# Layer 1 feed-forward of a decoder kernel: outer products of routes and ranks made transposed from PSUM

## The chip, the cores and the metric

The kernel runs on one core of a Trainium2 chip. A core has five engines with a queue each, worked off in order: PE multiplies matrices (its weight loads, PEld, are listed apart), DVE works on vectors, ACT applies functions, POOL (GpSimd) does general work, and SP issues transfers. The metric is the device time of one execution in microseconds, as the median over several runs.

## The reference

The program is a decoder with twelve steps: in each of four layers a mixer, a cross-attention or the like, and a feed-forward. `x` has 16 blocks of 128 tokens with 256 features. The change touches the sixth step alone, the feed-forward of Layer 1, which adds this to `x` (with the layer-normalised `x` as input):

```
TOPK = 4                                  # A: (64, 16, 256), B: (64, 256, 16), W: (256, 256)
vecs = jnp.einsum('arh,bsh->bsar', A, x)
arrows = jnp.linalg.norm(vecs, axis=-1)
_, idx = jax.lax.top_k(arrows, TOPK)
routes = jax.nn.one_hot(idx, arrows.shape[-1], dtype=x.dtype).sum(-2) / TOPK
v = jnp.einsum('bsa,bsar->bsr', routes, vecs)
delta = jnp.einsum('bsa,ajr,bsr->bsj', routes, B, v)
base = jnp.einsum('bsh,jh->bsj', x, W) + bias
return base + delta
```

For each token there are 64 routes of 16 ranks. The four routes with the longest vectors are chosen; their vectors are summed to `v`, and each chosen route sends `v` through its own matrix of B. So `delta` is one product of 1024 columns (64 routes by 16 ranks) with B, whose left side is the outer product of `routes` and `v`.

## The kernel before

`x` stays on the core, as 128 partitions (tokens) by 16 blocks by 256 features. A group is four blocks (`GB`), 512 tokens. `norm_T(g)` normalises a group and transposes it to `xT` (features on partitions) with PE's transposes and two copies.

`L1_ffn` (L680 to L743) works block by block, in two parts which `overlap` (L115) puts out one block apart: `route(i)`, then `expand(i-1)`.

- `route(i)` (L695): two products of 128x512 in PSUM, `pv`, from `xT` and A (L704). DVE copies them to `vecs` (L705), and ACT squares them to `sq` (L706). DVE sums the squares of each route to `n2` (L708), finds the eight largest and their places (L710, L712), and makes `rt`, a row of 64 zeros and ones (L716, L718). POOL multiplies `vecs` by `rt` (L720), DVE sums that over the routes to `v` (L722, L723), and writes the outer product of `rt` and `v` over `sq`, 128x1024 (L724).
- `expand(i)` (L727): PE transposes the outer product in eight parts to PSUM (`puT`, L732), ACT copies them to `uT` (L733), and one chain of products in PSUM, `pa`, adds W's part, the bias as a product with a row of ones, and eight products with B (L735). `add_x` (L150) adds `pa` to `x` on DVE.

Products of f32 operands appear in the profile as two records each: L92 is the line of the helper `chain` through which most products go, so they are told apart by their tiles. PSUM tiles come from three pools of banks: `mm` with four (`pv`), `tp` with two (all transposes), `ac` with two (`pa`). `vecs`, `sq` and `uT` have two buffers each.

The order of the instructions in each engine's queue isn't the source's order. A planner puts them out when they are ready by its own costs, with the source's order as priority, and inserts the waits. So instructions of neighbouring blocks, and some of the next step (`bn_stats` of Layer 2's first norm, loads of its weights), stand between those of this stage. The helper `Pipe` (L124), which holds back pieces of work for a number of steps, is there already and is used by Layer 2's mixer.

The next step, Layer 2's mixer (`mamba`, L765), starts with `norm_T(0)`, products `pconv` (L833), and small tables `cw`, `nw`, `vec` loaded at L781 to L787.

Of the kernel before, what the change touches and what calls it, by code (L numbers as in the profile page):

```python
# [11 lines left out]
F32 = mybir.dt.float32  # L12
BF16 = mybir.dt.bfloat16
# [4 lines left out]
ALU = mybir.AluOpType  # L18
# [4 lines left out]
P = 128  # L23
NB = 16
S = 128
D = 256
GB = 4
NG = NB // GB
GT = GB * S
# [12 lines left out]
class Decoder:  # L42
# [637 lines left out]
    def L1_ffn(self):  # L680
        nc = self.nc
        NA, R, TOP = 64, 16, 4
        wa = self.load_w("L1_fA", 2, NA * R)
        wb = self.load_w("L1_fB", 8, D)
        ww = self.load_w("L1_fWT", 2, D)
        with ExitStack() as es:
            pool = lambda n, b: es.enter_context(self.tc.tile_pool(name="l1f_" + n, bufs=b, reuse_waits="tile"))
            one, sm, big = pool("1", 1), pool("sm", 3), pool("big", 2)
            bias = one.tile([1, D], F32, tag="bias", name="bias")
            nc.sync.dma_start(bias, self.I["L1_fbias"])  # L690
            count = one.tile([P, NA], F32, tag="count", name="count")
            nc.gpsimd.iota(count, [[1, NA]], base=0, channel_multiplier=0, allow_small_or_imprecise_dtypes=True)
            of = lambda t: t.rearrange("p (a r) -> p a r", a=NA)

            def route(i):  # L695
                xT = self.norm_T(i // GB) if i % GB == 0 else self.l1_xT
                self.l1_xT = xT
                xj = [xT[:, k, self.cols(i % GB)] for k in range(2)]
                vecs = big.tile([P, NA * R], F32, tag="vecs", name="vecs")
                sq = big.tile([P, NA * R], F32, tag="sq", name="sq")  # L700
                for f in range(2):
                    fs = slice(512 * f, 512 * f + 512)
                    pm = self.psum("pv")
                    self.chain(pm, [(xj[k], wa[:, k, fs]) for k in range(2)])  # L704
                    nc.vector.tensor_copy(vecs[:, fs], pm)  # L705
                    nc.scalar.activation(sq[:, fs], pm, AF.Square)  # L706
                n2 = sm.tile([P, NA], F32, tag="n2", name="n2")
                nc.vector.tensor_reduce(n2, of(sq), AX.X, ALU.add)  # L708
                top = sm.tile([P, 8], F32, tag="top", name="top")
                nc.vector.max(top, n2)  # L710
                ix = sm.tile([P, 8], U32, tag="ix", name="ix")
                nc.vector.max_index(ix, top, n2)  # L712
                ixf = sm.tile([P, 8], F32, tag="ixf", name="ixf")
                nc.vector.tensor_copy(ixf, ix)
                rt = sm.tile([P, NA], F32, tag="rt", name="rt")
                nc.vector.tensor_scalar(rt, count, ixf[:, 0:1], None, ALU.is_equal)  # L716
                for k in range(1, TOP):
                    nc.vector.scalar_tensor_tensor(rt, count, ixf[:, k : k + 1], rt, ALU.is_equal, ALU.add)  # L718
                rb = rt.unsqueeze(2).broadcast_to([P, NA, R])
                nc.gpsimd.tensor_tensor(of(vecs), of(vecs), rb, ALU.mult)  # L720
                v = sm.tile([P, R], F32, tag="v", name="v")
                nc.vector.tensor_reduce(v, vecs.rearrange("p (a r) -> p r a", a=NA), AX.X, ALU.add)  # L722
                nc.vector.tensor_scalar(v, v, 1.0 / TOP**2, None, ALU.mult)  # L723
                nc.vector.tensor_tensor(of(sq), rb, v.unsqueeze(1).broadcast_to([P, NA, R]), ALU.mult)  # L724
                return xj, sq

            def expand(i, xj, u):  # L727
                uT = big.tile([P, 8, P], F32, tag="uT", name="uT")
                for f in range(2):
                    pt = self.psum_t("puT")  # L730
                    for k in range(4):
                        nc.tensor.transpose(pt[:, self.cols(k)], u[:, self.cols(4 * f + k)], self.ident)  # L732
                    nc.scalar.copy(uT[:, 4 * f : 4 * f + 4, :].rearrange("p k s -> p (k s)"), pt)  # L733
                pa = self.psum_a()
                self.chain(  # L735
                    pa[:, :D],
                    [(xj[k], ww[:, k, :]) for k in range(2)]
                    + [(self.ones[0:1, :], bias)]
                    + [(uT[:, k, :], wb[:, k, :]) for k in range(8)],
                )  # L740
                self.add_x(i, pa[:, :D])

            self.overlap(NB, route, expand)  # L743


    def softplus(self, pool, z):
# [957 lines left out]
```

## Time and profile before

| what | value |
|---|---|
| median of 3 runs (lowest, highest) | 2934.99 us (2932.88, 2945.16) |
| the profiled execution, time | 2938.75 us |
| the profiled execution, span | 2937.0 us |
| PE, DVE, ACT, POOL busy, share of the span | 86%, 53%, 30%, 28% |
| granted PE clock, mean over the span | 0.885 |
| first instruction on `vecs`, last on `uT` in this stage | 957.0, 1144.3 us |
| L722, sum over routes on DVE, 16 times | 1875 ns mean |
| L724, outer product on DVE, 16 times | 1293 ns mean |
| L708, sums of squares on DVE, 16 times | 1218 ns mean |
| L720, `vecs` by `rt` on POOL, 16 times | 1932 ns mean |
| L705, copy of `vecs` on DVE, 32 times | 682 ns mean |
| L706, square on ACT, 32 times | 604 ns mean |
| L733, copy of `uT` on ACT, 32 times | 591 ns mean |

A profile is one execution as the hardware recorded it. Busy time is what an engine spent in instructions; since matmuls are pipelined and their ends are modelled, a busy PE isn't a PE at its peak. A row of the timeline gives the start in us, the duration in us, the engine, the line, the operation, the tile written and the tiles read with their sizes, how many instructions were merged, and in brackets the idle time before it and what ended that. A row of the waits gives who waited for whom, the sum in us, how often, and the longest.

### The profile page before, as it was taken

Reading aid. Unit: us, or ns where it says so; the run is one execution under the profiler, and the core shown is the slowest. Engines: PE = TensorE matmul, PEld = TensorE weight load, DVE = VectorE, ACT = ScalarE, POOL = GpSimd, SP = SyncE. Lnnn points to the kernel's source line nnn. Section 1 sums busy time; section 2 is a strip of 40 time slices with the busy share of each in tenths; the row PEclk is TensorE's granted clock in tenths of the full one; section 3 lists DMA queues with packets and bytes.
Section 4 is the critical chain, followed back from the end, with each engine's and each line's share of the span. In section 5 each row is a group of like instructions: output and inputs, shape, how many; then the busy total and the mean of one; then the engine's idle time right before and its main releaser. Section 6 shows DMA issues by size and latency. Waiting matters only on the chain. (4 is left out here: it accounts for less than half of the span.)

```text
span 2937.0 us, 33648 instructions
## 1 busy us (share of the span) xinstructions
PE 2523.7 (86%) x12796; PEld 1617.7 (55%) x12796; DVE 1562.2 (53%) x3276; ACT 876.1 (30%) x1590; POOL 827.0 (28%) x880
## 2 busy tenths in 40 slices
PE   7778989989789888889888899399998885979986
PEld 4554444555444555445555566256755565756665
DVE  4998962477533777767676766712245652111110
ACT  1015551256344213433223333121134520111111
POOL 2630110034410212343356666000123314011111
PEclk9898889989788999889799999699888975989998
DMA  4000010000100001000000000200100022132221
GB/s 127 1 25 18 13 44 1 33 1 19 37 1 1 1 1 41 1 1 1 26 7 1 1 1 1 70 1 0 38 1 14 1 71 77 57 80 55 81 55 13
DMA packets 58143, 74.37 MB, mean 25 GB/s; under 512 B 7620, under 2 KB 49669, under 8 KB 57878
## 3 DMA queue, kind: packets, MB, share of 16 engines
q1 hardware_dynamic: 50678, 63.66, 7.0%
q0 software_dynamic: 7296, 8.48, 1.6%
q8 instruction: 103, 1.69, 0.3%
q14 instruction: 66, 0.54, 0.1%
HBM read 55.12 MB, written 18.04 MB: 25 GB/s over the span
## 5 line engine op out<-in xcount | busy, mean ns | idle before, releaser
L1590 POOL DMA_INDIRECT out_dram<-y,xe x40 | 61.9, 1549 | 383.1 <-ACT y L1589 295.9
L1581 DVE TENSOR_TENSOR hT<-sl,pgb 128x320 f32<-128x320 f32 x112 | 54.6, 487 | 194.8 <-PE pgb L92 194.8
L92 PE MATMUL pga<-xeT,e_w1T 128*128 128x320 f32 x448 | 142.4, 441 | 0.0
L92 PE MATMUL pgb<-xeT,e_w3T 128*128 128x320 f32 x448 | 139.8, 435 | 0.0
L92 PE MATMUL pa<-e_w2T,hT 128*128 128x256 f32 x560 | 126.0, 385 | 0.0
L92 PEld LDWEIGHTS pa<-e_w2T,hT 128*128 128x128 f32 x560 | 107.5, 193 | 14.7
L553 DVE TENSOR_TENSOR hT<-sl,pgb 128x512 f32<-128x512 f32 (+1 forms) x56 | 38.4, 686 | 143.0 <-PE pgb L92 137.5
L195 POOL COPY rs<-mv 128x4 f32<-128x4 f32 x48 | 10.8, 227 | 357.7 <-DVE mv L194 357.7
L92 PEld LDWEIGHTS pga<-xeT,e_w1T 128*128 128x128 f32 x448 | 87.0, 196 | 35.0 <-issue 1.4
L92 PEld LDWEIGHTS pgb<-xeT,e_w3T 128*128 128x128 f32 x448 | 86.1, 192 | 36.1 <-issue 1.2
L1580 ACT ACTIVATE sl<-pga 128x320 f32<-128x320 f32 x112 | 48.9, 437 | 190.6 <-PE pga L92 190.6
L1325 POOL TENSOR_TENSOR sc<-sc,mx 128x512 f32<-128x512 f32 x64 | 65.1, 1038 | 132.9 <-DVE mx L1324 81.3
L270 POOL TENSOR_TENSOR prod<-qkv 128x2048 f32<-128x2048 f32 (+7 forms) x24 | 78.0, 3257 | 67.9 <-DVE sc L271 59.8
L198 DVE TENSOR_SCALAR xn<-x,mv,rs 128x256 f32<-128x256 f32 x192 | 80.7, 469 | 28.1 <-POOL rs L102 28.0
L386 PE MATMUL ps<-qb,kT 32*128 32x512 f32 x256 | 80.6, 724 | 13.6 <-ACT pT L391 10.4
L1126 ACT ACTIVATE sc<-sc 128x512 f32<-128x512 f32 x64 | 40.3, 630 | 172.9 <-POOL sc L1125 172.9
L624 PE MATMUL ps<-qb,kn 32*128 32x256 f32 x512 | 87.6, 509 | 4.0 <-DVE kn L610 2.8
L92 PE MATMUL pconv<-xT,w_L_w 128*128 128x512 f32 (+1 forms) x192 | 87.5, 601 | 2.7 <-DVE mt L944 2.2
L1120 PE MATMUL ps<-kk,qq 128*128 128x128 f32 x512 | 73.6, 300 | 17.7 <-POOL qq L1066 17.7
L1120 PEld LDWEIGHTS ps<-kk,qq 128*128 128x128 f32 x512 | 68.1, 210 | 33.8 <-POOL qq L1066 18.7
L630 ACT ACTIVATE pT<-ps 128x512 f32<-128x512 f32 x128 | 67.8, 601 | 62.5 <-PE ps L624 62.4
L193 DVE BATCH_NORM_STATS2 st<-x 128x6 f32<-128x256 f32 x192 | 77.7, 413 | 15.3 <-DMA x<-in_x 6.5
(475 smaller groups left out, 6088.5 us busy)
## 6 DMA issues: line engine op xcount, KB each, us to landing
e_w1T<-in_L_w1T SPq DMA_DIRECT2D x8, 896.0 KB, 6.6
e_w3T<-in_L_w3T SPq DMA_DIRECT2D x8, 896.0 KB, 6.0
e_w2T<-in_L_w2T SPq DMA_DIRECT2D x8, 896.0 KB, 6.3
slots<-blank SPq DMA_DIRECT2D x8, 652.5 KB, 11.3
xe<-slots SPq DMA_DIRECT2D x8, 652.5 KB, 4.1
ct<-in_ctx SPq DMA_DIRECT2D x8, 512.0 KB, 4.6
x<-in_x SPq DMA_DIRECT2D x4, 512.0 KB, 6.6
ctx<-in_ctx SPq DMA_DIRECT2D x16, 128.0 KB, 2.3
```

The lines of the kernel that those rows point to most:

```text
L92: self.nc.tensor.matmul(out, a, b, start=(i == 0), stop=(i == n - 1))
L193: nc.vector.bn_stats(st[:, j, :], self.x[:, g * GB + j, :])
L198: nc.vector.tensor_scalar(xn[:, j, :], self.x[:, g * GB + j, :], mv[:, j, 0:1], rs[:, j : j + 1], ALU.subtract, ALU.mult)
L270: nc.gpsimd.tensor_tensor(prod[:, :k, :], qkv[:, m0 : m0 + k, 256:512], q, ALU.mult)
L386: nc.tensor.matmul(ps[r], kT[rw, j, c, :], qb[rw, j, c].rearrange("p e n -> p (e n)"), start=True, stop=True)
L624: nc.tensor.matmul(ps[r][:, D * c : D * c + D], kn[rw, j, self.cols(c)], qb[rw, j, e], start=True, stop=True)
L630: nc.scalar.activation(pT.rearrange("p c t -> p (c t)"), ps[r], AF.Exp, scale=5.0)
L1120: nc.tensor.matmul(ps[:, self.cols(n)], qq[n][e][:, cs], kk[e][:, cs], start=True, stop=True)
L1325: nc.gpsimd.tensor_tensor(sc, sc, mx.unsqueeze(2).broadcast_to([P, 4, S]), ALU.add)
L1580: nc.scalar.activation(sl, pa[:, :HALF], AF.Silu)
L1581: nc.vector.tensor_tensor(hT[:, f, hs], sl, pb[:, :HALF], ALU.mult)
L1590: nc.gpsimd.indirect_dma_start(out, bass.IndirectOffsetOnAxis(xe[:, t, D + 4 : D + 5].bitcast(I32), 0), y, None, bounds_check=NB * S - 1, ...
```

## The change

The outer product is no longer written with tokens on partitions and then transposed. Per group, `rt` (now bfloat16, kept for four blocks) and `v8` (v divided by 16, repeated eight times to 128 columns) are transposed to `rT` (64 routes by 512 tokens) and `vT` (128 by 512). For each of eight parts of the 1024 columns a product of `member`, a table of zeros and ones in bfloat16, with `rT` spreads eight routes over 128 partitions in PSUM, and DVE multiplies that by `vT` into `uT`. The pieces are held back by `Pipe` and put out over the four blocks after their group. The copies of `vecs` go from DVE to ACT. The bias is loaded to all partitions and added to `x` by POOL, one instruction a group, instead of being a product in each chain. `member` is made once at the stage's start by three POOL instructions.

```diff
-            bias = one.tile([1, D], F32, tag="bias", name="bias")
-            nc.sync.dma_start(bias, self.I["L1_fbias"])
+            bias = one.tile([P, 1, D], F32, tag="bias", name="bias")
+            nc.sync.dma_start(bias[:, 0, :], self.I["L1_fbias"][0].partition_broadcast(P))
+
+            whole = one.tile([NA, 8, 8, R], F32, tag="whole", name="whole")
+            nc.gpsimd.memset(whole, 1.0)
+            nc.gpsimd.affine_select(
+                out=whole, in_=whole, pattern=[[-8, 8], [-1, 8], [0, R]], compare_op=ALU.is_equal, fill=0.0, base=0,
+                channel_multiplier=1,
+            )
+            member = one.tile([NA, 8, P], BF16, tag="member", name="member")
+            nc.gpsimd.tensor_copy(member, whole.rearrange("p f k r -> p f (k r)"))
+            pipe, group = self.Pipe(), {}
...
             def route(i):
-                xT = self.norm_T(i // GB) if i % GB == 0 else self.l1_xT
-                self.l1_xT = xT
-                xj = [xT[:, k, self.cols(i % GB)] for k in range(2)]
+                if i % GB == 0:
+                    group["xT"] = self.norm_T(i // GB)
+                    group["rt"] = sm.tile([P, GB, NA], BF16, tag="rt", name="rt")
+                    group["v"] = sm.tile([P, GB, 8, R], F32, tag="v8", name="v8")
+                    xg = self.x[:, i : i + GB, :]
+                    nc.gpsimd.tensor_tensor(xg, xg, bias.broadcast_to([P, GB, D]), ALU.add)
+                rt, v8 = group["rt"][:, i % GB, :], group["v"][:, i % GB]
+                xj = [group["xT"][:, k, self.cols(i % GB)] for k in range(2)]
...
-                    nc.vector.tensor_copy(vecs[:, fs], pm)
+                    nc.scalar.copy(vecs[:, fs], pm)
                     nc.scalar.activation(sq[:, fs], pm, AF.Square)
...
-                rt = sm.tile([P, NA], F32, tag="rt", name="rt")
...
-                nc.vector.tensor_scalar(v, v, 1.0 / TOP**2, None, ALU.mult)
-                nc.vector.tensor_tensor(of(sq), rb, v.unsqueeze(1).broadcast_to([P, NA, R]), ALU.mult)
-                return xj, sq
-
-            def expand(i, xj, u):
-                uT = big.tile([P, 8, P], F32, tag="uT", name="uT")
-                for f in range(2):
-                    pt = self.psum_t("puT")
-                    for k in range(4):
-                        nc.tensor.transpose(pt[:, self.cols(k)], u[:, self.cols(4 * f + k)], self.ident)
-                    nc.scalar.copy(uT[:, 4 * f : 4 * f + 4, :].rearrange("p k s -> p (k s)"), pt)
...
-                    + [(self.ones[0:1, :], bias)]
...
-            self.overlap(NB, route, expand)
+                nc.vector.tensor_scalar(v8, v.unsqueeze(1).broadcast_to([P, 8, R]), 1.0 / TOP**2, None, ALU.mult)
+
+            def expand(g, xT, rt, v8):
+                rT = big.tile([NA, GT], BF16, tag="rT", name="rT")
+                vT = big.tile([P, GT], F32, tag="vT", name="vT")
+                uT = big.tile([P, 8, GT], F32, tag="uT", name="uT")
+
+                def turn():
+                    pt = self.tp.tile([NA, GT], BF16, tag="tp", name="prT")
+                    for j in range(GB):
+                        nc.tensor.transpose(pt[:, self.cols(j)], rt[:, j, :], self.identb)
+                    nc.scalar.copy(rT, pt)
+                    pv = self.psum_t("pvT")
+                    for j in range(GB):
+                        nc.tensor.transpose(pv[:, self.cols(j)], v8[:, j].rearrange("p k r -> p (k r)"), self.ident)
+                    nc.scalar.copy(vT, pv)
+
+                def outer(fs):
+                    for f in fs:
+                        pu = self.psum_t("pu")
+                        nc.tensor.matmul(pu, member[:, f, :], rT, start=True, stop=True)
+                        nc.vector.tensor_tensor(uT[:, f, :], pu, vT, ALU.mult)
+
+                def sums(js):
+                    for j in js:
+                        pa = self.psum_a()
+                        self.chain(
+                            pa[:, :D],
+                            [(xT[:, k, self.cols(j)], ww[:, k, :]) for k in range(2)]
+                            + [(uT[:, k, self.cols(j)], wb[:, k, :]) for k in range(8)],
+                        )
+                        self.add_x(g * GB + j, pa[:, :D])
+
+                pipe.put(1, turn)
+                pipe.put(2, lambda: outer(range(4)))
+                pipe.put(3, lambda: (outer(range(4, 8)), sums([0])))
+                pipe.put(4, lambda: sums([1, 2, 3]))
+
+            for i in range(NB):
+                route(i)
+                pipe.step()
+                if i % GB == GB - 1:
+                    expand(i // GB, group["xT"], group["rt"], group["v"])
+            pipe.drain()
```

More of the change, by code (lines that the diff above doesn't have):

```diff
@@ L722, in route @@
                 nc.vector.tensor_reduce(v, vecs.rearrange("p (a r) -> p r a", a=NA), AX.X, ALU.add)
-                nc.vector.tensor_scalar(v, v, 1.0 / TOP**2, None, ALU.mult)
-                nc.vector.tensor_tensor(of(sq), rb, v.unsqueeze(1).broadcast_to([P, NA, R]), ALU.mult)
-                return xj, sq
-            def expand(i, xj, u):
-                uT = big.tile([P, 8, P], F32, tag="uT", name="uT")
-                for f in range(2):
-                    pt = self.psum_t("puT")
-                    for k in range(4):
-                        nc.tensor.transpose(pt[:, self.cols(k)], u[:, self.cols(4 * f + k)], self.ident)
-                    nc.scalar.copy(uT[:, 4 * f : 4 * f + 4, :].rearrange("p k s -> p (k s)"), pt)
[L734 to L737, printed above, removed]
-                    + [(self.ones[0:1, :], bias)]
-                    + [(uT[:, k, :], wb[:, k, :]) for k in range(8)],
-                )
-                self.add_x(i, pa[:, :D])
```

## The prediction

> **What bounds the kernel now.** The page's chain of waits is followed back over 2% of the span only, so it doesn't reach the changed stage. I asked for the tiles vecs, uT and rt instead: all lie between 955 and 1145 us. The busy times of that stretch:
>
> ```profile
> core 0: us, PE busy (x) PEld busy (x) DVE busy (x) ACT busy (x) POOL busy (x), PEclk, DMA share, GB/s
> 955.00:1145.00 190.00, 162.50 (x638) 106.64 (x638) 139.18 (x291) 35.92 (x67) 42.42 (x37) 0.97 0.04 10
> ```
>
> PE looks 86% busy and DVE 73%; neither is full. Matmul rows overlap, so the PE sums below use distances between starts. Next, the waits of the stretch, of which two matter:
>
> ```profile
> DVE v L722 <- POOL vecs L720: 24.9, 14, 2.1
> ...
> PE puT L732 <- DVE sq L724: 18.9, 11, 2.9
> ```
>
> DVE stands for POOL's product, PE for DVE's outer product. One block's turn in the timeline shows both, first DVE:
>
> ```profile
> 1117.78 1.22 DVE L708 TENSOR_REDUCE n<-sq 128x64 f32<-128x1024 f32 x1 [1.02 <-ACT sq L706]
> ...
> 1120.12 0.92 DVE L718 SCALAR_TENSOR_TENSOR rt<-count,ixf,rt 128x64 f32<-128x64 f32 x3
> 1123.09 1.87 DVE L722 TENSOR_REDUCE v<-vecs 128x16 f32<-128x1024 f32 x1 [2.04 <-POOL vecs L720]
> 1124.88 0.41 DVE L152 TENSOR_TENSOR x<-x,pa 128x256 f32<-128x256 f32 x1
> 1125.20 0.17 DVE L723 TENSOR_SCALAR v<-v 128x16 f32<-128x16 f32 x1
> 1125.32 0.43 DVE L193 BATCH_NORM_STATS2 st<-x 128x6 f32<-128x256 f32 x1
> 1125.66 1.21 DVE L724 TENSOR_TENSOR sq<-rt,v 128x1024 f32<-128x1024 f32 x1
> 1126.79 1.28 DVE L705 COPY vecs<-pv 128x512 f32<-128x512 f32 x2
> 1127.98 0.17 DVE L194 BATCH_NORM_AGGREGATE mv<-st 128x2 f32<-128x6 f32 x1
> 1129.17 1.22 DVE L708 TENSOR_REDUCE n<-sq 128x64 f32<-128x1024 f32 x1 [1.02 <-ACT sq L706]
> ```
>
> and PE in the same time:
>
> ```profile
> 1118.11 3.72 PE L92 MATMUL pa<-w_L_fB,uT 128*128 128x256 f32 x16
> 1121.66 3.60 PE L92 MATMUL pv<-w_L_fA,xT 128*128 128x512 f32 x8
> 1127.02 1.06 PE L732 MATMUL puT<-ident,sq 128*128 128x128 f32 x8 [1.76 <-DVE sq L724]
> 1127.92 1.03 PE L92 MATMUL pa<-w_L_fWT,xT 128*128 128x256 f32 x4
> 1128.88 0.69 PE L92 MATMUL pa<-bias,ones 1*128 1x256 f32 x2
> 1129.50 0.48 PE L92 MATMUL pa<-w_L_fB,uT 128*128 128x256 f32 x1
> ```
>
> A block takes 1129.17 - 1117.78 = 11.39 us. DVE: routing 3.3 us, idle 2.0, the rest 5.1, idle 1.0: 8.3 busy, and 8.8 with the xT copy and the four xn of each group (0.68 + 1.37 us, a quarter each). PE, start to start: 3.55 (B product) + 3.43 (vecs; its next start from another turn, 1050.88 to 1054.31) + 0.90 + 0.96 + 0.62 = 9.46, and 9.7 with xT's transposes (1.04 a group). So the stage is a ring, not an engine at its limit: PE's transposes need DVE's sq, DVE's next n2 needs PE's next pv, and all stand while POOL multiplies. Any relief of one part alone would be eaten; loosening the ring is what can pay.
>
> **The change, part by part**, for one block (16 in the stage, 4 in a group).
>
> *Off DVE:* sq's outer product, 1.13 us by starts, and two copies of vecs, 1.19. ACT takes these copies: L706's square of the same 128x512 takes 0.60, so +1.2, while ACT loses two uT copies (L733, 0.59 each). ACT was busy 35.92 of 190 us; I cost it at nothing. If it had no room it would be 1.2 us a block.
>
> *On DVE:* eight products of PSUM and vT a group. The nearest row is L553, PSUM times SBUF at the same 128x512: 0.686. 8 x 0.686 / 4 = 1.37. The wider v8 (128x128, as L758: 0.23) instead of L723's 0.17: +0.06. DVE: 8.8 - 2.3 + 1.4 = 7.9.
>
> *PE:* minus bias 0.62 and eight f32 transposes 0.90. Plus, per group, four transposes of v8 and four of rt, 0.11 each as before's eight in 0.90, and eight member products of 128x512 in bf16. **Row against rule:** the trace has no such product. Its nearest row is pv: f32, 512 columns, two records of 0.43, 0.86 in all. The Trainium skill (TensorE: Matmul & The Clock Gate, Wait — 56ns, not 53.3ns?) gives 216 ns for a bf16 matmul of 512 columns at the full clock; the granted clock here is 0.97. By the row the 32 products cost 27.5 us, by the rule 6.9. I take the rule, since pv's 0.86 is four times it and f32 records come in pairs; the row's end, +20.6 us, stays for the range. PE: 9.7 - 1.5 + (1.73 + 0.88) / 4 = 8.85, or 142 us for 16.
>
> *Bias on POOL:* one 128x1024 add a group, as L720 at 1.93; 7.7 in all, and POOL is busy 42 of 190 us. memset, affine_select and copy for member come first: 0.95 (L823), 2.0 at most (L1276, twice the width), 1.05 (L1472), in 24.9 us of POOL idleness ahead of L692. L195's norm of group 1 sits behind them, but its xn isn't used until 993. add_x waits for the bias, queued one group earlier: nothing. **A rule against it:** SBUF — State Buffer (SBUF: two separate sides) says that DVE operations with two SBUF inputs, or in a 2-port mode, and GpSimd's exclude each other. The trace agrees: sq at 970.92 took 2.49 instead of 1.21 beside POOL's product, L714's cast once 1.79 instead of 0.17; add_x, with one input in PSUM, kept its 0.42 at 1051.08. By the rule each add may hold DVE for up to 1.6 us, 6.4 in all; by the rows mostly nothing, as the long operations left (n2 and v reductions, products from PSUM) have one SBUF input. I take 2, inside the losses below. The bias on DVE would be 4 x 1.21 = 4.8, so the exchange is near even.
>
> *The ring:* sq is now free right after n2, and the products of group g run one to four blocks after its routes. So PE can run pv two blocks ahead (four banks, two vecs), and DVE has the next n2 and the last group's products for the 2 us of POOL's wait. Late next is PE: 142 us against 16 x 7.9 = 127.
>
> *What grouping costs:* at the start the first sums wait for seven routes (on DVE 3.3 + 1.8 + 0.2 and the norms' 0.5, 5.8 each) and eight products (5.5): 46 us after the first n2 at 960, at 1006. PE has by then nine pv (31), three xT (3) and the spreading (3): 37 of 51 us, 14 idle. At the end the last group's eight products (5.5) precede its four sums of 4.5 us: 5 idle.
>
> *SP:* the bias load (issued at 951 us) becomes 128 rows of 1 KB, needed by the first add_x: hidden. cw, nw and vec of the next layer were issued at 1135.13 behind ukv, which waits for the W weights (last W matmul 1133.06, ten us before the end). Now the last W matmul comes some 4 us before the end; cw (3.5 us to issue) is wanted 4.5 us after it (L840): 0 to 3 us, I take 0.
>
> **Sum.** PE 142 + 14 + 5, and 5 for remaining waits (0.4 in each of the 12 blocks after the first group, where before had 1.9): 166 instead of 190. Span 2937 - 24 = 2913. The profiled run took 2938.75, 1.75 more than its span; the median of the runs is 2934.99, so **2911**. Its own range: PE losses between 0 with 8 at the head (153, 2898) and 1.0 a block plus 6.4 of holding and 3 of SP (182, 2927).
>
> **Rivals.** *A: ideal overlap.* PE full but for the tail, 147: 2892. For it: the ring is gone. Against it: the first group has no sums to give PE.
>
> *B: bursts.* The sums of steps 3 and 4, 18 us, stand ahead of the next pv, and DVE runs dry. A group then takes three routes and eight products on DVE (3 x 5.8 + 5.5 = 23), 4 for the next pv and its squares, and the 18: 45. Head 4 x 5.8 + 4 = 27, three groups 135, tail 2 + 5.5 + 18 = 26: 188, so 2933, no change. bf16 products at the f32 row's pace (so not doing what is intended) land near, 2911 + 20.6 = 2932. Against it: the trace shows half of a later block's pv (1012.86) put ahead of an earlier block's B product (1013.82).
>
> *C: slower, by the two tp banks.* The third product of each half-group needs the first's bank back; if DVE's multiplication stands behind a whole route with POOL's wait, 3.3 + 2.0 + 1.8 = 7.1 us, PE, which works in order, stops with pv behind it. With 1.4 for the two following, 8.5 twice a group is 68 us: 142 + 68 + 5 = 215, +25: 2960. It beats before from about 7 us of stop a group. For it: PE's wait on sq is this kind of wait. Against it: queues here are filled by readiness, not in the source's order.
>
> **Numbers.** Mine 0.58, A 0.10, B 0.16, C 0.16. Runs of this kernel can tell about 0.5%, 14.7 us. Faster by that: 0.50 of mine and A: 0.60; same: 0.08 of mine and B: 0.24; slower: C, 0.16. The range runs from A, 2892, over mine and B to 2944, which takes in B with some 10 us more loss; C and what lies below A, about 0.2, stay out.
>
> **What would show it.** The stage's end moves from 1145 to about 1121; puT and its wait are gone; DVE's wait for L720 falls from 24.9 to under 8; PE holds about 10 us of waits on DVE's products, near the end of the stage and at its first group. C shows as PE standing for uT or at pu products in every group, B as DVE idle before n2 while sums run. Wrong would be me if the queues' order puts pv behind the sums, or if what is saved here returns as a wait in Layer 2's first blocks.

## The result and the profile after

The changed kernel takes 2906.74 us (median of 6 runs, 2903.29 to 2919.63) beside 2936.17 us (6 runs) for the kernel before in the same comparison: a ratio of 0.9905 with a 95% interval of 0.9884 to 0.9926. The profiled execution took 2903.98 us, its span is 2902.2 us. Repeated later, the ratio was 0.9907 (0.9873 to 0.9941).

In all that follows "the stage" runs from the start of the first `pv` product on PE to the end of the sixteenth and last `add_x`. It took 955.02 to 1145.16 = 190.1 us before and 952.83 to 1117.29 = 164.5 us after. Its busy times, in the columns of the prediction's first view (PE, PEld, DVE, ACT, POOL, then the granted clock):

```profile
952.83:1117.29 164.46, 152.14 (x543) 90.59 (x543) 129.00 (x282) 39.42 (x76) 49.68 (x43) 0.98 0.03 9
```

Some 25.7 us went, but PE is busy only 10 us less than the 162.5 of before: the larger part of what went, 15 us, is time in which it stood. The waits of this stretch (who waited for whom, sum in us, times, longest):

```profile
DVE v L736 <- POOL vecs L734: 14.5, 11, 2.1
...
PE pu L759 <- DVE uT L760: 4.2, 7, 1.0
PE pv L92 <- DVE xT L86: 4.0, 2, 3.2
```

L736 is the old L722 and L734 the old L720. DVE stood 24.9 us for POOL before and stands 14.5 now, although POOL's product still takes 1.92 us: in five of 16 blocks DVE had something else to do meanwhile. PE's 18.9 us of waiting for `sq` are gone with `puT`; nothing as large took their place. The first group in PE's timeline (start, duration, operation; idle time before it in brackets):

```profile
952.83 14.00 PE L92 MATMUL pv<-w_L_fA,xT 128*128 128x512 f32 x32
...
969.47 1.12 PE L92 MATMUL pv<-w_L_fA,xT 128*128 128x512 f32 x2 [1.33 <-ACT xT L84]
973.76 5.47 PE L92 MATMUL pv<-w_L_fA,xT 128*128 128x512 f32 x6 [3.17 <-DVE xT L86]
...
993.08 0.39 PE L759 MATMUL pu<-rT,member 64*128 64x512 bf16 x1
993.39 0.70 PE L92 MATMUL pa<-w_L_fB,uT 128*128 128x256 f32 x2
```

PE runs four blocks of `pv` at once (952.83), then depends on DVE. The first product with B starts at 993.39, not after all eight parts are done: the planner puts one spreading product and one piece of a sum in turn. The last group shows how little the grouping costs there:

```profile
1098.64 0.39 PE L759 MATMUL pu<-rT,member 64*128 64x512 bf16 x1
1098.96 0.70 PE L92 MATMUL pa<-w_L_fB,uT 128*128 128x256 f32 x2
1099.59 0.39 PE L759 MATMUL pu<-rT,member 64*128 64x512 bf16 x1
...
1108.04 1.03 PE L92 MATMUL pa<-w_L_fWT,xT 128*128 128x256 f32 x4
...
1112.35 1.03 PE L92 MATMUL pa<-w_L_fWT,xT 128*128 128x256 f32 x4
```

`pu` comes every 0.95 us with a piece of a sum between, and a whole sum takes 4.31 us (1108.04 to 1112.35), back to back.

### The profile page after: what moved, and what is told of

Its sections match the earlier page's. It is cut to its first block, busy times and chain, and to the rows that moved or that the text cites. A ratio compares the mean times of both kernels' runs of the same rounds, so it can differ in the third digit from the quotient of the medians.

```text
span 2902.2 us, 33424 instructions
## 1 busy us (share of the span) xinstructions
PE 2504.8 (86%) x12700; PEld 1595.4 (55%) x12700; DVE 1550.5 (53%) x3260; ACT 879.6 (30%) x1598; POOL 837.8 (29%) x887
## 5 line engine op out<-in xcount | busy, mean ns | idle before, releaser
L198 DVE TENSOR_SCALAR xn<-x,mv,rs 128x256 f32<-128x256 f32 x192 | 83.7, 484 | 30.4 <-POOL rs L102 30.3
L84 ACT COPY xT<-pt 128x512 f32<-128x512 f32 x40 | 23.5, 587 | 224.4 <-PE pt L230 222.8
L1159 PEld LDWEIGHTS ps<-kk,qq 128*128 128x128 f32 x512 | 67.5, 209 | 33.7 <-POOL qq L1105 18.7
```

The lines of the kernel that those rows point to most:

```text
L198: nc.vector.tensor_scalar(xn[:, j, :], self.x[:, g * GB + j, :], mv[:, j, 0:1], rs[:, j : j + 1], ALU.subtract, ALU.mult)
L1159: nc.tensor.matmul(ps[:, self.cols(n)], qq[n][e][:, cs], kk[e][:, cs], start=True, stop=True)
```

## The experiments

Two theories stood at the start. **T1**, the prediction's: PE and DVE stand in a ring, so it must be loosened as a whole. **T2**: DVE's own chain sets the pace, and taking work from DVE pays by itself. In the later runs T1 and T2 are the two that each expectation names. The table has every run; the ratio is to the kernel before, measured beside it, with its 95% interval. "Lost to the clock" is an estimate from each profile: summed over stretches of 1 us of the stage, PE's busy time times what the granted clock lacks to 1. The mixer's time runs from the stage's end to the start of the mixer's last addition to `x`.

| kernel | median us | ratio | stage us | lost to the clock, us | Layer 2's mixer us |
|---|---|---|---|---|---|
| before | 2936.17 | 1 | 190.1 | 5.0 | 352.5 |
| changed kernel | 2906.74 | 0.9905 (0.9884 to 0.9926) | 164.5 | 2.7 | 343.8 |
| after_again | 2904.85 | 0.9907 (0.9873 to 0.9941) | 164.5 | 2.6 | 347.3 |
| copies_on_act | 2915.75 | 0.9935 (0.9910 to 0.9959) | 175.0 | 1.7 | 350.6 |
| bias_on_pool | 2933.09 | 0.9997 (0.9978 to 1.0017) | 186.7 | 7.9 | 352.5 |
| copies_and_bias | 2912.83 | 0.9936 (0.9920 to 0.9953) | 172.0 | 5.0 | 350.0 |
| after_dve_copies | 2916.02 | 0.9950 (0.9933 to 0.9966) | 174.4 | 6.1 | 344.2 |
| after_bias_on_pe | 2906.27 | 0.9913 (0.9896 to 0.9930) | 170.5 | 1.7 | 348.1 |
| after_bias_on_dve | 2906.20 | 0.9915 (0.9898 to 0.9931) | 162.5 | 0.0 | 348.8 |
| after_f32_spread | 2920.87 | 0.9949 (0.9920 to 0.9977) | 182.6 | 4.3 | 350.0 |
| after_no_hold | 2965.85 | 1.0110 (1.0094 to 1.0127) | 232.4 | 33.7 | 344.0 |
| after_short_hold | 2914.71 | 0.9914 (0.9884 to 0.9945) | 174.3 | 10.0 | 344.0 |
| after_first_group_halved | 2906.72 | 0.9911 (0.9883 to 0.9939) | 166.2 | 3.4 | 348.9 |
| after_halved_bias_on_dve | 2904.47 | 0.9879 (0.9825 to 0.9932) | 166.8 | 3.2 | 337.7 |

The stage is read from one profiled execution each; it repeats to 0.1 us in the changed kernel. The mixer doesn't (343.8 and 347.3), so a difference of a few us in the total says little about the stage. Nor does a difference of 2 us between two stages say much: in all these profiles the clock stands at 1.00 or at 0.50, at 0.50 within the stage for 3.41 us or a whole multiple of it, and one such stretch is worth some 1.7 us.

### The parts, one by one, in the kernel before

**copies_on_act.** Only the two copies of `vecs` go to ACT:

```diff
-                    nc.vector.tensor_copy(vecs[:, fs], pm)
+                    nc.scalar.copy(vecs[:, fs], pm)
```

> Before, with only the two copies of vecs moved from DVE to ACT; all else as before. The stage (first pv to last add into x) took 190.1 us before and 164.5 after. Theory 1, the prediction's: the ring of PE and DVE has to be loosened by taking the outer product out of it, and a relief of DVE alone is eaten by waits: the stage stays at 182 us or more, the total gains under 9 us. Theory 2: in the turn that the prediction quotes, DVE's own chain is the whole ring (n2, rt, POOL, v, sq, copies, ACT's square, n2 again), and PE only waits beside it; without the copies (1.19) and the wait for ACT (1.02) a block falls from 11.39 to PE's 9.7: stage 163 to 170 us, total 20 to 27 us less than before, so this small edit alone is worth most of the change.

Measured: 175.0 us, between the two. This one line brings 15.1 of the 25.6 us, 0.94 us a block of the 1.19 taken from DVE. Some 3.3 of the 15.1 are the clock (5.0 us lost to it before, 1.7 here). What still stands, in the waits of its stage:

```profile
DVE v L722 <- POOL vecs L720: 32.7, 16, 2.1
...
PE puT L732 <- DVE mv L194: 10.1, 7, 1.9
...
PE puT L732 <- DVE sq L724: 2.9, 5, 1.1
```

DVE now waits for POOL in every one of the 16 blocks, where it did in 14: it comes to that point sooner and has nothing else to do. PE's wait for the outer product is 13.0 us here, since L194 follows L724 directly in DVE's queue and is named in its place in seven of 12; before it was 18.9 and a further 3.8 named L194. So T1's "eaten" is refuted, and T2's full gain didn't come either; that DVE waits about 8 us longer for POOL is the likely reason.

**bias_on_pool.** Only the bias moves, from the chain to GpSimd:

```diff
...
+                if i % GB == 0:
+                    xg = self.x[:, i : i + GB, :]
+                    nc.gpsimd.tensor_tensor(xg, xg, bias.broadcast_to([P, GB, D]), ALU.add)
...
-                    + [(self.ones[0:1, :], bias)]
```

> Before, with only the bias moved from PE's chain to one POOL addition a group. Theories 1 and 2: PE isn't the limit, so its 0.62 us a block become slack, and POOL's additions can hold DVE: stage 188 to 196 us, total within 6 us of before. Theory 3, that PE's time is what counts: 16 x 0.62 = 10 us less, stage 180.

Measured: 186.7 us, 3.4 less than before, between T3's 180 and the 188 of the others, although PE is spared 16 x 0.62 = 9.9. Some 2.9 of the difference is the clock (7.9 us lost to it, 5.0 before). The total is unchanged. The stage began 12 us later there (967.29), and what shows there is the clock, not the edit: from 800 to 940 us, in the step ahead, it was granted at 0.74 and not at 0.83, worth some 12 us.

**copies_and_bias.** Both of these diffs together:

> Before, with the copies on ACT and the bias on POOL, but the outer product and its transposes as before. Theory 1: stage 180 us or more. Theory 2: PE's limit falls to 9.1 us a block: stage 153 to 163 us, as good as the whole change or better.

Measured: 172.0 us, between the two again. The parts add up: 15.1 + 3.4 = 18.5 against 18.1. So of the 25.6 us the outer product made from PSUM brings the last 7.5 (172.0 to 164.5), of which some 2.4 are the clock.

### One part taken back, in the changed kernel

**after_dve_copies.** `vecs` is copied by DVE again:

```diff
-                    nc.scalar.copy(vecs[:, fs], pm)
+                    nc.vector.tensor_copy(vecs[:, fs], pm)
```

> After, with the copies of vecs back on DVE. DVE then has 7.9 + 1.2 = 9.1 us a block against PE's 8.85. Theory 1: the ring stays loose, DVE becomes the limit with the same head and tail: stage 170 to 177 us. Theory 2: nearly all of the gain is given back: 183 us or more.

Measured: 174.4 us, +9.9 (3.4 of it the clock), as T1 had it. The same edit is worth 15.1 us in the old ring and 9.9 in the loosened one. Without the copies' move the rest of the change brings 186.7 - 174.4 = 12.3 over bias_on_pool, against 7.5 with it: each part does some of what the other does.

**after_bias_on_pe.** The bias returns as a product with a row of ones:

```diff
...
-                    nc.gpsimd.tensor_tensor(xg, xg, bias.broadcast_to([P, GB, D]), ALU.add)
...
+                            + [(self.ones[0:1, :], bias)]
```

> After, with the bias back as a product in PE's chain and no addition on POOL. The stage took 164.5 us after. If PE is the limit of the new stage (theory 1), 16 x 0.62 = 10 us come back, less some 3 us in the first group where POOL's additions held DVE's xn and cast: stage 169 to 175 us. Theory 2, that POOL's holding of DVE costs as much as the bias saved on PE: stage 164 us or less.

Measured: 170.5 us, +6.0 of the 9.9 us that PE gets back to do, T1's case. The total doesn't show it (2906.27 against 2906.74): the profiled stage is longer, the median isn't.

**after_bias_on_dve.** The same addition, on DVE instead of GpSimd:

```diff
-                    nc.gpsimd.tensor_tensor(xg, xg, bias.broadcast_to([P, GB, D]), ALU.add)
+                    nc.vector.tensor_tensor(xg, xg, bias.broadcast_to([P, GB, D]), ALU.add)
```

> After, with the four additions of the bias on DVE instead of POOL. On DVE 4 x 1.2 = 4.8 us; on POOL they took 2.34 each and held DVE's xn, cast and rt beside them. Theory 1, an even exchange: stage 161 to 168 us. Theory 2, that the holding matters in the first group, where DVE is the limit: 160 us or less.

Measured: 162.5 us, -2.0, as T1 had it, and no more than the clock's 2.7; the total is the same. GpSimd's addition is not free for DVE. In the changed kernel, both engines in one timeline:

```profile
976.80 2.04 POOL L734 TENSOR_TENSOR vecs<-vecs,rt 128x1024 f32<-128x1024 f32 x1 [6.04 <-DVE top L725]
...
977.32 1.55 DVE L729 CAST ixf<-ix 128x8 f32<-128x8 uint32 x1
...
978.81 2.34 POOL L711 TENSOR_TENSOR x<-x,bias 128x1024 f32<-128x1024 f32 x1
978.90 2.29 DVE L730 TENSOR_SCALAR rt<-count,ixf 128x64 bf16<-128x64 f32 x1
```

The cast of eight numbers a partition ends 0.03 us after POOL's product, the comparison of 64 ends 0.05 us after POOL's addition. By groups in the stage of the changed kernel (line, engine, operation, shapes, count; busy time, mean ns):

```profile
L730 DVE TENSOR_SCALAR rt<-count,ixf 128x64 bf16<-128x64 f32 x16 | 9.8, 615 | 0.4
L711 POOL TENSOR_TENSOR x<-x,bias 128x1024 f32<-128x1024 f32 x4 | 9.3, 2344 | 0.0
...
L729 DVE CAST ixf<-ix 128x8 f32<-128x8 uint32 x16 | 6.6, 410 | 0.3
```

and with the addition on DVE:

```profile
L711 DVE TENSOR_TENSOR x<-x,bias 128x1024 f32<-128x1024 f32 x4 | 7.0, 1746 | 0.7 <-DMA bias<-in_L_fbias 0.7
...
L730 DVE TENSOR_SCALAR rt<-count,ixf 128x64 bf16<-128x64 f32 x16 | 6.5, 407 | 0.3
...
L729 DVE CAST ixf<-ix 128x8 f32<-128x8 uint32 x16 | 2.6, 165 | 0.2
```

DVE does the additions itself in 7.0 us and has 7.3 us less in these two small operations, and 3.5 us less in `xn` (from 10.1 us for 18 to 5.8 for 16 in the same view, the two more at 0.41). Over the whole stage it is busy 126.8 us instead of 129.0: the exchange is nearly even.

**after_f32_spread.** `member`, `rt` and `rT` in f32 instead of bfloat16:

```diff
-            member = one.tile([NA, 8, P], BF16, tag="member", name="member")
+            member = one.tile([NA, 8, P], F32, tag="member", name="member")
...
-                rT = big.tile([NA, GT], BF16, tag="rT", name="rT")
+                rT = big.tile([NA, GT], F32, tag="rT", name="rT")
...
```

> After, with member, rt and rT in float32, so that the 32 spreading products are f32. Each would take 0.86 us as the pv row does, where the bfloat16 one took 0.32 from its start to the next: 17 us more on PE. Theory 1, PE the limit: stage 176 to 183 us. Theory 2, PE has idle time to take them: 170 us or less.

Measured: 182.6 us, +18.1, T1's case. The spreading products, first in the changed kernel, then here (count; ns least, median, most):

```profile
L759 PE MATMUL pu<-rT,member x32: 372/386/387, 986.0 to 1102.4; 64*128 64x512 bf16 x32
```

```profile
L759 PE MATMUL pu<-rT,member x64: 589/589/693, 984.0 to 1115.4; 64*128 64x512 f32 x64
```

One record a product in bfloat16, two in f32. The durations overlap with what follows; by starts a bfloat16 product takes 0.32 us and an f32 one 1.05 alone (1044.33 to 1045.38) or 0.96 in a row of two (1035.30 to 1037.21). The difference, 0.64 to 0.73 us, times 32 is 20 to 23, of which the stage shows 18.1 (1.6 of it the clock; the sixteen transposes of `rt` are f32 here too). So this choice of a type is worth more than the outer product's whole part.

### The hold of `Pipe`

**after_no_hold.** The pieces of a group are put out as soon as it is complete:

```diff
-                pipe.put(1, turn)
-                pipe.put(2, lambda: outer(range(4)))
-                pipe.put(3, lambda: (outer(range(4, 8)), sums([0])))
-                pipe.put(4, lambda: sums([1, 2, 3]))
+                turn()
+                outer(range(8))
+                sums(range(GB))
```

> After, with a group's transposes, products and sums put out at once behind its last route, not held back over four blocks. Theory 1: the hold is what lets PE and DVE run apart; without it each group's products and sums stand ahead of the next routes, some 7 us of stop a group: stage 185 us or more. Theory 2: the planner orders by readiness anyway, and only the grouping counts: stage within 5 us of 164.5.

Measured: 232.4 us and slower than before, ratio 1.0110, on T1's side and far beyond its 7 us of stop a group. The same operations lose 68 us of the profiled stage by their order alone, and 59 us of the median (the profiled execution was the slowest of its four). The next expectation's "220" ends this stage at the first of the last four `add_x` (1170.08); the last ends at 1182.26. PE's waits in the stage, the stage's busy times, and three stretches of its first group:

```profile
PE pvT L753 <- DVE v L737: 36.1, 12, 4.0
PE prT L749 <- DVE rt L732: 8.4, 9, 1.8
```

```profile
949.88:1182.26 232.38, 181.21 (x543) 103.59 (x543) 129.93 (x282) 40.42 (x76) 50.23 (x43) 0.77 0.02 6
```

```profile
965.00:975.00 10.00, 2.81 (x12) 1.70 (x12) 7.99 (x16) 3.07 (x7) 3.82 (x2) 0.88 0.00 0
975.00:995.00 20.00, 13.72 (x27) 5.69 (x28) 9.93 (x20) 1.16 (x2) 1.91 (x1) 0.50 0.00 1
995.00:1010.00 15.00, 14.76 (x68) 12.45 (x67) 4.83 (x14) 0.58 (x1) 0.46 (x3) 0.95 0.00 0
```

PE works its queue in order and stands 44.5 us at transposes of `rt` and `v` that DVE hasn't made, with the next group's norm and `pv` behind them. Then the second loss: with this idleness the granted clock (third number from the end) falls to 0.50, and a spreading product with its piece of a sum takes 1.69 us (985.37 to 987.06) where it takes 0.95 in the changed kernel. The clock is at 0.50 in each of the four groups, for 24 to 27 us. By the sum used in the table the stage loses 33.7 us to the clock here, and 2.7 in the changed kernel; PE is not busy for 51.2 us against 12.3. These two (+31.0 and +38.9) make 69.9, against 67.9 measured.

**after_short_hold.** Each piece but `turn` is put out one block earlier than in the change:

```diff
-                pipe.put(2, lambda: outer(range(4)))
-                pipe.put(3, lambda: (outer(range(4, 8)), sums([0])))
-                pipe.put(4, lambda: sums([1, 2, 3]))
+                pipe.put(1, lambda: outer(range(4)))
+                pipe.put(2, lambda: (outer(range(4, 8)), sums([0])))
+                pipe.put(3, lambda: sums([1, 2, 3]))
```

> The changed kernel with each piece of a group held one block less: turn and the first four member products one block after the group, the rest and the first sums two, the last sums three. In the changed kernel PE stands 14.3 us before the first sums, 63 us into the stage. T1, the first group's wait is what is left to gain and two or three blocks of hold are enough to keep PE's queue free: the first sums come one block of DVE's routing (5.8 us) earlier, stage 157 to 162. T2, the hold is needed at its full length, since the transposes and products of a group otherwise reach PE before DVE has made the routes and products they read, with pv behind them, as in the kernel without a hold (220): stage 168 or more.

Measured: 174.3 us, in T2's range, but hardly by T2's story, in which `pv` stands behind. The start gained, though little: the third group's transposes of `xn`, the first PE work after the first group's sums, come 61.65 us after the stage's start (1009.13) and not 63.21. All was lost in the last group, in stretches of the end:

```profile
1089.00:1094.00 5.00, 0.62 (x2) 0.20 (x2) 2.77 (x6) 0.58 (x1) 3.56 (x8) 0.91 0.29 74
1094.00:1098.00 4.00, 2.61 (x5) 0.88 (x5) 2.50 (x5) 0.71 (x2) 0.17 (x1) 0.50 0.00 0
1098.00:1110.00 12.00, 12.00 (x25) 6.21 (x25) 4.70 (x9) 0.00 (x0) 1.84 (x2) 0.50 0.00 0
```

PE had done the earlier groups' sums and stood some 6 us for the last routes, with no `pv` left to hold up; then it ran 12 us and more at half clock. By the sum used above the clock costs 10.0 us here, 7.3 more than in the change, and PE isn't busy 3.8 us more: 11.1, against 9.9 measured. The sums held back from the third group are what keeps PE busy until DVE has finished the fourth.

### The start of the stage

**after_first_group_halved.** The first group alone is expanded in two halves of two blocks:

```diff
...
-                if i % GB == GB - 1:
+                if i in (1, 3):
+                    expand(0, group["xT"], group["rt"], group["v"], i - 1, 2)
+                elif i % GB == GB - 1:
                     expand(i // GB, group["xT"], group["rt"], group["v"])
```

> The changed kernel with the first group alone expanded as two halves of two blocks (256 columns a product), so that its first sums need two routes and not four. It adds eight member products and eight multiplications on DVE at half the width, and leaves the hold as it is. T1, PE's 14.3 us of idleness at the stage's start can be filled by earlier sums: the first sums come some 11 us earlier, the stage takes 155 to 160, and the median falls some 6 us below the changed kernel's. T2, DVE is what limits the first 60 us (its routes and norms fill it), and earlier sums only move PE's idleness behind them, with the added products (8 x some 0.45 us on DVE) on top: stage 163 to 168.

Measured: 166.2 us, T2's case. The first product with B starts 22.2 us into the stage (975.88), not 40.6, yet the third group's transposes of `xn` come at 62.98 us instead of 63.21. Filling PE's early gaps only moved them; DVE is busy 54.3 of these 63.0 us.

**after_halved_bias_on_dve.** The same with the addition on DVE (the diff of after_bias_on_dve).

> As the kernel before, the first group in halves, with the bias addition on DVE instead of GpSimd (four instructions of some 1.2 us). T1, PE's early idleness is the loss and DVE has slack after the first group: the stage is within 2 us of the halved kernel's, as the same exchange moved the changed kernel's by 2. T2, DVE limits the first group: the two additions that stand in it, with GpSimd's hold of DVE gone, shift the stage by 3 us or more from the halved kernel's.

Measured: 166.8 us, T1's case, 0.6 from the halved kernel. This doesn't settle what bounds the start: the exchange is nearly even for DVE, as after_bias_on_dve shows, so it would hardly move a stage that DVE limits either. Its ratio, 0.9879, is the lowest of all, but its interval takes in all others near 0.991: no version was shown to beat the change.

### What follows the stage

The profiled spans differ by 34.8 us, more than the stage. Most of the rest is Layer 2's mixer, which the change doesn't touch. First before, then after:

```profile
1145.16:1497.66 352.50, 310.11 (x2020) 174.84 (x2020) 245.39 (x475) 126.64 (x186) 127.26 (x163) 0.87 0.04 10
```

```profile
1117.29:1461.09 343.80, 303.83 (x2020) 170.81 (x2020) 244.04 (x467) 126.42 (x185) 127.38 (x163) 0.89 0.04 12
```

PE has the same 2020 records, at a granted clock of 0.87 and 0.89. Is that the change's doing? The changed kernel was run once more, unaltered:

> The changed kernel once more, unaltered, to see whether what follows the stage repeats. In the changed kernel's first profile Layer 2's mixer took 343.8 us at a mean granted clock of 0.89, in the kernel before 352.5 at 0.87, with the same instructions. T1, the mixer's granted clock is set by the order in which the kernel's queues bring work to PE: stage 163 to 166, mixer 343 to 345 and 0.89 again. T2, it is chance of one execution: the stage repeats, and the mixer lands anywhere from 338 to 353. The median over the runs should be within 6 us of 2906.7 in either case.

The stage repeated (164.5), the mixer took 347.3 us at 0.88, outside what T1 allowed: so T2, at least in part. Over all kernels the mixer's time goes with its clock: 352.5 at 0.87 down to this, of after_halved_bias_on_dve:

```profile
1122.60:1460.30 337.70, 298.05 (x2020) 168.79 (x2020) 244.57 (x467) 126.42 (x185) 127.46 (x163) 0.91 0.04 12
```

There too the clock is 1.00 or 0.50. Before, the mixer holds 92.2 us at 0.50, 27 stretches of 3.41; the changed kernel 22, its repetition 24, this last one 18. Less half of these times, the mixer takes 304 to 307 us in every kernel, so its differences are these stretches nearly alone. What decides how many there are wasn't found. The medians, 29.4 us apart, fit the stage's 25.6 with some 4 us of this.

## Why the prediction was right, point by point

The forecast was 2911 us, measured 2906.74; for the stage 166 us, measured 164.5. The mechanism, a loosened ring in which PE's work and its head decide, holds in the main (after_f32_spread, after_bias_on_pe); that the sum came so close is partly luck, since several terms missed and made up for each other:

- **"Any relief of one part alone would be eaten": wrong**, and the main step of reasoning that failed. The copies alone brought 15.1 us. The ring did pass DVE's relief on: a shorter DVE turn brings `sq` and so the next `puT` forward too. It took back only a part, through POOL's wait. That all parts together reach the forecast doesn't depend on it, since the sum was made from the end state.
- **PE's work, 142 us.** Measured by starts 139.9: sums 16 x 4.31 = 69.0, `pv` 16 x 3.43 = 54.9, spreading 10.1, transposes of routes and `v` 3.3, of `xn` 2.6. The spreading was taken at 6.9; that is made up for by the sums, for which 16 x 4.51 = 72.2 was taken (the old chain was broken up by the bias), and by `xn`, of which only three groups fall into the stage.
- **The bfloat16 product by the rule, 0.216 us** (the Trainium skill, TensorE: Matmul & The Clock Gate, Wait — 56ns, not 53.3ns?). Between f32 products, as most of them stand, it takes 0.32 by starts (1098.64 to 1098.96); of two in a row (1026.46 to 1026.99, 0.53) the second adds 0.21, as the rule has it. The 32 cost 10.1 us and not 6.9. The row of f32 `pv` would have been wrong by far, 27.5; after_f32_spread shows what that end costs, +18.1 where +20.6 was worked out.
- **Idleness of PE, 24 us.** Measured by the same starts 164.5 - 139.9 = 24.6. The head has 14.3 of it (14 predicted, though the first sums came in pieces at 993 and not at 1006, so the match is partly luck), the middle two groups 8.0, or 1.0 a block for which 0.4 was taken, and the tail 2.2 instead of 5, since products and sums interleave. Not all of it is standing: PE's busy record lacks only 12.3 us (8.4, 3.9 and 0.0). The rest is the half clock and somewhat longer steps where kinds of products alternate.
- **DVE under POOL's wait.** DVE's wait for the product was to fall from 24.9 to under 8 and fell to 14.5: in 11 of 16 blocks DVE still had nothing else to do. The sum didn't rest on that: DVE's work was forecast at 127 us and is 129.0. PE's waits on DVE's products were 4.2, where 10 were expected.
- **The bias on GpSimd.** An addition takes 2.34 us, for which L720's 1.93 was used. Its holding of DVE was taken as 2 us of at most 6.4; the bound was too low, as 10.8 us of DVE's time (7.3 and 3.5) went when the additions were moved. The excess over the usual times in L729, L730 and L198 of the changed kernel adds up to about 12 us (6.6 - 16 x 0.17, 9.8 - 16 x 0.25, 10.1 - 18 x 0.41), from POOL's product as well as its addition. The estimate was saved, by luck, by where it falls: moved to DVE, the additions changed the stage by 2.0, and there the clock stayed at 1.00 through the head, where the changed kernel loses 2.7 us to it after a gap: the likely cause of the 2.0, not a tested one. "The long operations left have one input" was true, and short ones with one input were held instead: the prediction's own row, the cast of 1.79, was such a one. The additions on DVE took 1.75 each, where 1.21 was taken.
- **At nothing: copies on ACT, `member`'s setup, SP.** ACT is busy 39.4 of 164.5 us. The setup took 0.95 + 1.53 + 1.03 and lay ahead of the stage. `cw`, `nw` and `vec` were issued at 1080.74 to 1082.83, 35 us before the stage's end: the planner put them ahead of `ukv`, so the feared 0 to 3 us were 0.
- **Rivals.** A, PE full but for the tail, fails by the 24.6 us of idleness. B, bursts with DVE dry, doesn't show: sums and `pv` alternate within a block. C, the two `tp` banks, shows only as 4.2 us of waiting for `uT` in seven places, 1.0 at the longest. Its mechanism, PE held by one early instruction with `pv` behind it, is real: after_no_hold has it, at the transposes, for a stage 42 us longer than before.
- **The range.** Its own lower end, 153, doesn't follow from its terms: 142 of work, 8 at the head and the tail's 5 make 155, so 2900 and not 2898.

## What to carry to other kernels

Before calling two engines a ring in which single reliefs are lost, move one cheap operation off one of them and measure: here one line gave 59% of the stage's gain, some of it by the clock. Where a batch of late work is put into an in-order queue, hold it back until its inputs are surely there, and keep enough of it in hand for the end, since PE pays twice for standing, in the wait and in the clock after it. Between products of f32, a product of zeros and ones belongs in bfloat16.

## What the runs showed of the hardware

**The clock after a gap.** In the changed kernel PE stood from 970.6 to 973.8 us; the granted clock fell from 1.00 to 0.50 at 972.3 and was back at 979.1, after 5.3 us of unbroken `pv` products. In after_short_hold it fell at 1093.1 and stayed at 0.50 through 8.4 us (1096.95 to 1105.39) of single bfloat16 products in turn with two f32 records, though PE shows as busy throughout; it returned at 1110.1, 4.7 us after an unbroken run of sums began. In after_no_hold the same: an unbroken run from 992.65, full clock at 996.5, 3.8 us later. In the stages of all these profiles a time at 0.50 lasts 3.41 us or 2, 5, 7 or 8 times that, so a return comes only at such a step, here at the end of the first one that lies wholly within an unbroken run. A mixture of small products seems not to bring the clock back, though it doesn't lower it either: the same mixture kept 1.00 in the changed kernel from 1095.27 to 1102.75. That was seen, not tested by itself.

**GpSimd and small DVE operations.** A DVE operation of 64 numbers a partition that usually takes 0.25 us took 2.29 beside a GpSimd addition, ending 0.05 us after it; it is not only the large operations with two inputs that are held. With the additions on DVE, the mean of this operation fell from 615 to 407 ns and that of the cast from 410 to 165.
